# Expert blocks of a mixture-of-experts layer in pairs: first products and gelus of two blocks in one step, second products of both in the next

## The chip, the cores and the metric

The kernel runs on one core of a Trainium2 chip, as one program. The metric is the device time of one execution in microseconds (us), the median of the runs shown. Below, PE is TensorE (matrix products), DVE is VectorE, ACT is ScalarE, POOL is GpSimd and SP is SyncE, which here issues DMAs.

## The reference, cut to what matters

Two transformer layers run over x, 4 rows of 1024 tokens of width 128, in float32. The first layer (multi-query attention and a switched-head layer) is not touched by the change and fills the time up to about 2850 us. The second is:

```python
xn = _layernorm(x, axis=-1)
x = x + _L1_attn_ref(xn, ...) + _L1_ffn_ref(xn, ...)

def _favorp(data, proj, is_query):          # FAVOR attention, 16 heads, 64 features
    ...
    data_dash = jnp.einsum('bhnd,hjd->bhnj', data_normalizer * data, proj)
    diag = jnp.sum(data * data, axis=-1, keepdims=True) * (0.5 * data_normalizer * data_normalizer)
    ...                                      # stab: a maximum over the features
    return ratio * jnp.exp(data_dash - diag - stab) + EPS_FEAT

def _L1_ffn_ref(x, ...):                     # 8 experts, 2 per token, HID = 512
    logits = xf @ gate_w + gate_b
    top_w, top_i = jax.lax.top_k(logits, K)
    ...
    for e in range(E):
        h = jax.nn.gelu(xf @ w1[e] + b1[e], approximate=False)
        out = out + combine[:, e:e + 1] * (h @ w2[e] + b2[e])
    shared = jax.nn.gelu(xf @ ws1 + bs1, approximate=False) @ ws2 + bs2
    return (out + shared).reshape(orig_shape)
```

So ACT computes exps for the attention and gelus for the experts in the same stretch, and each change from one to the other needs an ACT_TABLE_LOAD.

## The kernel before, in words

**The work of the second layer.** A router has sorted the tokens by expert into blocks of 256 slots; there are 39 of them (NBLK). Of one block `j` five pieces are issued, all of them functions inside `experts()` (L1717):

- `load(j)`: SP issues the DMAs of the block's tokens xg (L1719 on) and of its expert's first weight w1. `load_second(j)`: the same of the second weight w2. All three have three buffers each.
- `turn(j)`: PE turns xg around into a PSUM tile xgT (L1739, 2 instructions), DVE copies it to SBUF (L1741), and POOL copies the columns that tell each slot's token and gate (whose, L1743; 6 buffers).
- `one(j)`: the first products pb (L1751, 8 instructions, into two PSUM tiles), and on ACT four gelus hb (L1757), two per PSUM tile. xgT and hb have two buffers each.
- `two(j)`: the second products pe (L1766, 16 instructions, one PSUM tile), two scalings yb on DVE by the gate (L1772), and two scatter-adds on POOL (L1776).

**The attention beside it.** `favor_keys(b)` (L1410) and `favor_queries(b)` (L1537) are generators, one pair per batch row. The keys: projections kp, qp (L1376), values v1p and their sum vs (L1433), diagonals dg (L1443), vsum (L1455), four groups ddk_0 to ddk_3 (L1391), the maximum over the row mxT and stab (L1481, L1488), va scaled by an exp (L1496, L1500), the products kv (L1509) and their transpose kvt (L1530). The queries: four groups ddq_0 to ddq_3, their transposes qt (L1560) with copies qfT on DVE and ACT (L1567, L1569), the outputs fo (L1578, oTf on DVE), ot (L1595), oT1p (L1614) and o1w (L1621). A group, ddq or ddk, is 16 instructions on PE into four PSUM tiles. DVE then takes four maxima of them (mq at L1545, mk at L1469) and four subtractions (qE, kE at L1401), and ACT one exp of 2048 columns (L1403).

**PSUM.** All these tiles come from one pool of eight banks of 512 columns (`small`, L76), given out in turn: a tile waits until its bank's earlier owner was read for the last time.

**The order.** In this layer PE and SP keep the order of the program (`manual_schedule`, L1214); for ACT, DVE and POOL the compiler's scheduler chooses it. The program's order is made by a loop at the end (L1818 on). It steps through the attention of row 0's keys, then row 0's queries with row 1's keys, and so on to row 3's queries, five phases in all. Each step of these generators adds a rate to `due`, and for each full 1.0 one step of a filler is issued between. The filler `fill()` (L1810) is: 13 steps of the shared expert (`shared(0, 6)`: ph with gelus, py, yT) for the first six tiles of 512 tokens, the rest of the last row of the layer before, then `experts()`, then five steps of the shared expert for the last two tiles. Behind the loop comes what is left of the filler. Last, the scatter-added sums are loaded (y) and added to x, and x is stored.

**Before the change** `experts()` has 78 steps: in iteration `j` it issues `load(j)`, `turn(j-1)`, `load_second(j-1)` and `one(j-2)` in one step, and `two(j-3)` in the next. The rates are 0.84, 0.5, 0.5, 0.5 and 1.2. With 40 attention steps in each of the three middle phases (20 of the keys and 20 of the queries), 20 filler steps, so ten blocks, go into each.

Of the kernel before, what the change touches and what calls it, by code (L numbers as in the profile page):

```python
# [58 lines left out]
NBLK = 2 * SLOTS // MB + ME - 1  # L59
# [12 lines left out]
def two_layers(ctx: ExitStack, tc: tile.TileContext, a: dict, out: bass.AP):  # L72
# [13 lines left out]
    def small(name):  # L86
        return banks.tile([P, 512], F32, tag="small", name=name)
# [262 lines left out]
    with ExitStack() as l0:  # L350
# [687 lines left out]
        def run(it):  # L1038
            for _ in it:
                pass  # L1040
# [676 lines left out]
    def experts():  # L1717
        rows_of = sorted_x.rearrange("(k q p) d -> k p q d", q=MB // P, p=P)
        loaded, seconds, turned, hidden, whose = {}, {}, {}, {}, {}  # L1719

        def load(j):
            at = nc.sync.value_load(block[0:1, 1, j : j + 1], min_val=0, max_val=ME * PER)
            xg = ff.tile([P, MB // P, ROW], F32, tag="xg", name=f"xg{j}", bufs=3)
            nc.sync.dma_start(xg, rows_of[ds(at, 1)].rearrange("o p q d -> p (o q) d"))
            e = nc.sync.value_load(block[0:1, 0, j : j + 1], min_val=0, max_val=ME - 1)
            w1 = ff.tile([P, MH], F32, tag="w1", name=f"w1_{j}", bufs=3)
            nc.sync.dma_start(w1, a["w1"][ds(e, 1)].rearrange("o d m -> d (o m)"))
            loaded[j] = xg, w1

        def load_second(j):  # L1730
            e = nc.sync.value_load(block[0:1, 0, j : j + 1], min_val=0, max_val=ME - 1)
            w2 = ff.tile([P, MHC, D], F32, tag="w2", name=f"w2_{j}", bufs=3)
            nc.sync.dma_start(w2, a["w2"][ds(e, 1)].rearrange("o (c p) d -> p (o c) d", p=P))
            seconds[j] = w2

        def turn(j):
            pt = small(f"xgT{j}")
            for q in range(MB // P):
                nc.tensor.transpose(pt[:, ts(q, P)], loaded[j][0][:, q, 0:D], ident)  # L1739
            turned[j] = ff.tile([P, MB], F32, tag="xgT", name=f"xgT{j}")  # L1740
            nc.vector.tensor_copy(turned[j], pt[:, 0:MB])  # L1741
            whose[j] = ff.tile([P, MB // P, 2], F32, tag="whose", name=f"whose{j}", bufs=6)
            nc.gpsimd.tensor_copy(whose[j], loaded[j][0][:, :, D:ROW])  # L1743

        def one(j):
            w1, xT = loaded.pop(j)[1], turned.pop(j)
            hT = hidden[j] = ff.tile([P, MHC, MB], F32, tag="hb", name=f"hb{j}")
            for c2 in range(MHC // 2):
                ph = small(f"pb{j}_{c2}")
                for k in range(2):  # L1750
                    nc.tensor.matmul(  # L1751
                        ph[:, ts(k, MB)], lhsT=w1[:, ts(2 * c2 + k, P)], rhs=xT,
                        start=True, stop=True,
                    )
                for k in range(2):
                    c = 2 * c2 + k
                    nc.scalar.activation(  # L1757
                        hT[:, c, :], ph[:, ts(k, MB)], AF.Gelu, bias=b1s[:, j, c : c + 1]
                    )

        def two(j):
            w2, hT, to = seconds.pop(j), hidden.pop(j), whose.pop(j)
            py = small(f"pe{j}")
            for q in range(MB // P):
                for c in range(MHC):
                    nc.tensor.matmul(  # L1766
                        py[:, ts(q, D)], lhsT=hT[:, c, ts(q, P)], rhs=w2[:, c, :],
                        start=(c == 0), stop=(c == MHC - 1),
                    )
            yb = ff.tile([P, MB // P, D], F32, tag="yb", name=f"yb{j}", bufs=3)  # L1770
            for q in range(MB // P):
                nc.vector.tensor_scalar(  # L1772
                    yb[:, q, :], py[:, ts(q, D)], to[:, q, 1:2], None, ALU.mult
                )

                nc.gpsimd.indirect_dma_start(  # L1776
                    out=sums[q][:, :],
                    out_offset=bass.IndirectOffsetOnAxis(
                        ap=to[:, q, 0:1].bitcast(I32), axis=0
                    ),  # L1780
                    in_=yb[:, q, :], in_offset=None, compute_op=ALU.add,
                )

        for j in range(NBLK + 3):
            if j < NBLK:
                load(j)
            if 0 <= j - 1 < NBLK:
                turn(j - 1)
            if 0 <= j - 1 < NBLK:
                load_second(j - 1)  # L1790
            if 0 <= j - 2 < NBLK:
                one(j - 2)
                yield
            if 0 <= j - 3 < NBLK:
                two(j - 3)
                yield

    def run(*its):

# [10 lines left out]
    def fill():  # L1810

        yield from shared(0, SOON)
        for _ in aside:
            pass
        yield from experts()
        yield from shared(SOON, B * T // TC)
# [1 line left out]
    filler = fill()  # L1818
    due, taken = 0.0, 0
    for k, (rows_now, rate) in enumerate((  # L1820
        ((0,), 0.84), ((0, 1), 0.5), ((1, 2), 0.5), ((2, 3), 0.5), ((3,), 1.2),
    )):
        its = [favor_queries(rows_now[0])] if k else [favor_keys(0)]
        its += [favor_keys(b) for b in rows_now[1:]]
        for _ in run(*its):
            for _ in range(3 if taken < 15 else 2):
                next(aside, None)
                taken += 1
            due += rate
            while due >= 1.0:  # L1830
                due -= 1.0
                next(filler, None)
# [78 lines left out]
```

## Time and profile before

| what | us |
|---|---|
| runs of the kernel before | 3313.93, 3315.99, 3317.91 |
| their median | 3315.99 |
| the profiled execution's own time | 3320.57 |
| its span, first to last instruction | 3318.8 |
| busy in the span: PE, DVE, ACT, POOL | 3156.9, 2413.3, 1850.8, 1899.0 |
| mean granted clock of TensorE | 0.976 |
| the stretch of the expert blocks, 2956 to 3286: length, PE busy, DVE busy, ACT busy | 330.00, 308.98, 268.09, 218.94 |
| behind it, 3286 to 3318.8: length, PE busy | 32.80, 24.65 |

How to read it: busy time is that of instructions that compute or copy; waits and DMA issues are not counted. The granted clock is the share of full speed that the throttle let TensorE have. A group of instructions is written with its line, engine, operation, and out<-in by the names in the program; behind it stand their number, busy time, mean ns of one, and the idle time of the engine just before them with what ended it. The profiled execution took 4.58 us more than the median of the runs.

### The profile page before, as it was taken

How to read it: one execution, taken by the hardware profiler on the slowest of the kernel's cores; microseconds unless marked ns; L12 is line 12 of the kernel's file. 1: busy time of each engine (PE TensorE's matmuls, PEld its weight loads, DVE VectorE, ACT ScalarE, POOL GpSimd, SP SyncE). 2: the span in 40 equal slices, each digit the busy share in tenths (PEclk: the TensorE clock that was granted, in tenths of full speed). 3: DMA queues.
4: the chain of work that ended last, by engine and by line, in shares of the span. 5: the costliest groups of instructions: out<-in, count | busy, mean ns of one | idle time of the engine just before them, and what ended most of it. 6: DMA issues, size and time to landing. Idle time of an engine off the chain costs nothing. (4 is left out here: it accounts for less than half of the span.)

```text
span 3318.8 us, 48971 instructions
## 1 busy us (share of the span) xinstructions
PE 3156.9 (95%) x15323; PEld 1714.7 (52%) x15323; DVE 2413.3 (73%) x4670; ACT 1850.8 (56%) x3273; POOL 1899.0 (57%) x2345
## 2 busy tenths in 40 slices
PE   6899999999999999999899999999999999789998
PEld 3354545555545444555454445555455554457776
DVE  7797777767777867676868776777666645658886
ACT  3345555565555555665455555656565566246675
POOL 2565555566657666666477667665767644123333
PEclk8999999999999999999999999999999999989999
DMA  5134443432323223333133232332323220024446
GB/s 152 43 97 132 132 141 98 120 108 87 94 70 99 83 79 92 95 90 90 58 95 89 84 100 83 104 87 85 93 87 93 87 76 13 12 66 89 88 88 136
DMA packets 458696, 299.77 MB, mean 90 GB/s; under 512 B 42490, under 2 KB 431108, under 8 KB 458436
## 3 DMA queue, kind: packets, MB, share of 16 engines
q1 hardware_dynamic: 412692, 225.32, 24.2%
q0 software_dynamic: 42976, 70.26, 7.7%
q8 instruction: 122, 2.00, 0.2%
q10 hardware_dynamic: 2768, 1.07, 0.1%
q14 instruction: 138, 1.13, 0.1%
HBM read 179.83 MB, written 116.26 MB: 89 GB/s over the span
## 5 line engine op out<-in xcount | busy, mean ns | idle before, releaser
L620 DVE TENSOR_REDUCE nmh<-mx 128x1 f32<-128x512 f32 x1024 | 663.8, 681 | 287.8 <-PE mx L614 286.2
L675 ACT ACTIVATE pT<-sT 128x512 f32<-128x512 f32 x1024 | 557.1, 600 | 157.6 <-PE sT L668 88.2
L874 POOL DMA_INDIRECT sorted_v<-xv,gates x464 | 469.9, 1013 | 228.0 <-DMA sorted_v<-xv,gates 129.5
L826 POOL TENSOR_TENSOR g_o<-g_o 128x256 f32<-128x256 f32 x256 | 189.4, 740 | 577.8 <-DVE g_o L825 545.6
L955 DVE TENSOR_REDUCE nms<-ps 128x1 f32<-128x1024 f32 x256 | 310.9, 1215 | 259.7 <-ACT ps L953 258.8
L950 PE MATMUL ss<-xnT,qTs 128*128 128x512 f32 x1024 | 493.2, 604 | 3.6 <-ACT qTs L820 2.0
L982 PE MATMUL cp<-pTs,vs 128*128 128x512 f32 x1024 | 460.8, 604 | 17.4 <-DVE pTs L974 11.5
L1003 PE MATMUL po<-ow,cTs 128*128 128x512 f32 x1024 | 473.1, 594 | 0.7 <-ACT cTs L987 0.7
L953 ACT COPY ps<-ss 128x512 f32<-128x512 f32 x512 | 299.3, 586 | 217.3 <-PE ss L950 213.8
L957 ACT ACTIVATE ps<-ps,nms 128x1024 f32<-128x1024 f32 x256 | 294.5, 1150 | 140.9 <-DVE nms L955 139.6
L1007 DVE TENSOR_TENSOR g_o<-po,go 128x512 f32<-128x512 f32 x512 | 333.6, 682 | 28.3 <-PE po L1003 14.1
L614 PE MATMUL mx<-ks,qs 72*128 72x512 bf16 x1024 | 312.9, 383 | 10.1 <-DVE nmh L620 4.0
L982 PEld LDWEIGHTS cp<-pTs,vs 128*128 128x128 f32 x1024 | 193.1, 194 | 243.2 <-issue 224.3
L668 PE MATMUL sT<-qs,ks 75*128 75x512 bf16 x1024 | 310.3, 383 | 7.3 <-DVE nmh L620 4.7
L950 PEld LDWEIGHTS ss<-xnT,qTs 128*128 128x128 f32 x1024 | 190.6, 192 | 182.3 <-issue 105.7
L970 PE MATMUL pTp<-ident,ps 128*128 128x128 f32 x2048 | 271.3, 275 | 13.2 <-ACT ps L957 8.8
L970 PEld LDWEIGHTS pTp<-ident,ps 128*128 128x128 f32 x2048 | 240.7, 142 | 79.6 <-issue 15.6
L926 POOL DMA_INDIRECT vs<-yv,gates x232 | 228.9, 987 | 67.4 <-issue 57.8
L926 POOL DMA_INDIRECT yg<-yv,gates x232 | 225.3, 971 | 73.4 <-issue 68.3
L987 ACT COPY cTs<-cp 128x512 f32<-128x512 f32 x64 | 37.5, 585 | 406.2 <-PE cp L982 406.2
L1003 PEld LDWEIGHTS po<-ow,cTs 128*128 128x128 f32 x1024 | 179.0, 191 | 158.3 <-issue 126.5
L658 PE MATMUL ov<-pT,va 128*32 128x512 f32 x2048 | 248.5, 603 | 0.0
(321 smaller groups left out, 4816.5 us busy)
## 6 DMA issues: line engine op xcount, KB each, us to landing
vb<-in_v_w_dram SPq DMA_DIRECT2D x667, 64.0 KB
xs<-sorted_v SPq DMA_DIRECT2D x145, 256.0 KB
yv<-xs SPq DMA_DIRECT2D x145, 256.0 KB
w<-in_w_dram SPq DMA_DIRECT2D x78, 256.0 KB
sorted_x<-nobody SPq DMA_DIRECT2D x16, 1040.0 KB
ow<-in_o_w_dram SPq DMA_DIRECT2D x32, 512.0 KB
qs<-qd SPq DMA_DIRECT2D x144, 64.0 KB
sorted_v<-xv,gates POOLq DMA_INDIRECT x464
```

The source lines that it names most:

```text
L614: nc.tensor.matmul(sc, lhsT=qs[0:NPAIR, i, ts(n, P)], rhs=ks[0:NPAIR, ts(kc, 512)], start=True, stop=True,)
L620: nc.vector.tensor_reduce(halves[:, i, n, kc : kc + 1], sc, axis=AX.X, op=ALU.max)
L668: nc.tensor.matmul(sc, lhsT=ks[:, ts(kt, P)], rhs=qs[:, i, ts(c, 512)], start=True, stop=True,)
L675: nc.scalar.activation(pT, sc, AF.Exp)
L874: nc.gpsimd.indirect_dma_start(out=sorted_v[u % 4][:, :], out_offset=bass.IndirectOffsetOnAxis(ap=column(u, k, n).bitcast(I32), axis=0), i ...
L926: nc.gpsimd.indirect_dma_start(out=to[:, n, :], out_offset=None, in_=unit[u, "y"][:, :], in_offset=bass.IndirectOffsetOnAxis(ap=column(u, ...
L950: nc.tensor.matmul(sc, lhsT=qT[:, ts(n, P)], rhs=xnT[b][:, ts(c, 512)], start=True, stop=True)
L955: nc.vector.tensor_reduce(nm, p, axis=AX.X, op=ALU.max, negate=True)
L970: nc.tensor.transpose(pt[:, ts(k, P)], p[:, ts(4 * k4 + k, P)], ident)
L982: nc.tensor.matmul(cp, lhsT=v[:, kt, :], rhs=pT[:, kt, :], start=(kt == 0), stop=(kt == NT - 1),)
L1003: nc.tensor.matmul(po, lhsT=cT[:, ts(qt, P)], rhs=unit[u, "ow"][:, ts(c, 512)], start=True, stop=True,)
L1007: nc.vector.tensor_tensor(g[:, ts(c, 4), :], po.rearrange("p (e c) -> p e c", e=4), bcast(go[:, ts(c, 4)], P), ALU.mult,)
```

## The change

The blocks are now issued in pairs. Ahead of the loop stand the loads of blocks 0 and 1, two empty steps, and a step with the turns of both. A round for blocks `j` and `j+1` has two steps. The first: `load(j+2)`, both first products with their gelus, `load(j+3)`, `load_second(j+2)`. The second: both second products, `load_second(j+3)`, and the turns of `j+2` and `j+3`. With 20 rounds (the last has one block) there are 43 steps instead of 78, and the rates of the last four phases are halved, so that ten blocks go into each middle phase as before. The buffers are as they were.

```diff
-        for j in range(NBLK + 3):
-            if j < NBLK:
-                load(j)
-            if 0 <= j - 1 < NBLK:
-                turn(j - 1)
-            if 0 <= j - 1 < NBLK:
-                load_second(j - 1)
-            if 0 <= j - 2 < NBLK:
-                one(j - 2)
-                yield
-            if 0 <= j - 3 < NBLK:
-                two(j - 3)
-                yield
+
+        def each(step, *js):
+            for j in js:
+                if 0 <= j < NBLK:
+                    step(j)
+
+        each(load, 0, 1)
+        each(load_second, 0, 1)
+        yield
+        yield
+        each(turn, 0, 1)
+        yield
+        for j in range(0, NBLK, 2):
+            each(load, j + 2)
+            each(one, j, j + 1)
+            each(load, j + 3)
+            each(load_second, j + 2)
+            yield
+            each(two, j, j + 1)
+            each(load_second, j + 3)
+            each(turn, j + 2, j + 3)
+            yield
...
-        ((0,), 0.84), ((0, 1), 0.5), ((1, 2), 0.5), ((2, 3), 0.5), ((3,), 1.2),
+        ((0,), 0.84), ((0, 1), 0.25), ((1, 2), 0.25), ((2, 3), 0.25), ((3,), 0.6),
```

## The prediction

> **What bounds the kernel now.** I read the page's first part, then the windows of the second layer, then PE's waits, its groups and the timelines. The edit touches only the stretch in which the 39 expert blocks run, 2956 to 3286 us. There PE (TensorE) is busy 308.98 of 330 us, DVE 268.09, ACT 218.94. It repeats a pattern of about 90 us, one per batch row (the third group of query products, ddq_2, starts at 2995.50, 3086.82 and 3176.56). Cut in two, two such patterns read, columns being stretch, length, busy time (instructions) of PE, PEld, DVE, ACT, POOL, granted clock, DMA:
>
> ```profile
> 2997.00:3042.00 45.00, 40.71 (x291) 30.30 (x290) 40.11 (x79) 33.98 (x40) 13.35 (x12) 0.90 0.34 72
> 3042.00:3087.00 45.00, 42.90 (x418) 37.24 (x421) 35.66 (x85) 25.84 (x39) 21.06 (x18) 1.00 0.48 105
> 3087.00:3132.00 45.00, 41.23 (x308) 30.46 (x309) 40.55 (x80) 34.23 (x40) 14.06 (x14) 0.92 0.36 73
> 3132.00:3177.00 45.00, 42.91 (x420) 37.23 (x422) 35.48 (x84) 25.84 (x39) 21.17 (x18) 1.00 0.48 105
> ```
>
> In the first half ("DVE half": ddq_2 to the last key group) PE and DVE are both nearly full, and PE runs below full clock; in the second ("PE half") PE alone is full. ACT is full in neither. Where PE stands still is in its waits (total us, times, longest):
>
> ```profile
> PE pe L1766 <- DVE xgT L1741: 6.3, 3, 2.1
> PE xgT L1739 <- ACT qfT L1569: 4.6, 3, 2.5
> PE ddk L1391 <- DVE qE L1401: 2.6, 3, 1.0
> PE pb L1751 <- DVE kE L1401: 2.4, 4, 0.7
> PE xgT L1739 <- DMA xg<-sorted_x: 1.6, 1, 1.6
> PE ot L1595 <- ACT hb L1757: 1.2, 2, 0.6
> ```
>
> Some 22 us of idle in all, half of it ended by DVE; gelus (hb) end 2.3. The groups that the edit aims at (busy, mean ns, idle before):
>
> ```profile
> L1757 ACT ACTIVATE hb<-pb,b1s 128x256 f32<-128x256 f32 x156 | 62.9, 473 | 43.3 <-PE pb L1751 42.9
> L1757 ACT ACT_TABLE_LOAD x32 | 41.1, 1283 | 22.6 <-PE pb L1751 22.4
> L1403 ACT ACT_TABLE_LOAD x28 | 35.9, 1283 | 11.7 <-issue 11.3
> ```
>
> ACT waits for PE before gelus (42.9 us), not PE for gelus.
>
> **Part 1, fewer table loads.** In the compiled order, the loads at L1403 and L1757 fall from 31 + 32 to 22 + 23 (not to 20: a pair's gelus are still split by an exp in places). 18 x 1.283 = 23.1 us of ACT leave. Of PE's idle time, ACT ends 4.6 (qfT) + 2.3 (hb) = 6.9 us. But the qfT copies are late because their exp waits for DVE ("ACT qE L1403 <- DVE qE L1401" is 26.5 us in ACT's waits), and the load in front of it is over before: at 3087.28 one starts, 4.68 of idle follow, then the exp. Bounds 0 and -6.9; I take 0.6 a pattern for three patterns, the size of one hb wait: **-1.8**.
>
> The Trainium skill, "ScalarE: Activation LUTs", "Rules for kernel authors", says to group functions by table set, as this edit does, and to budget about 2.7 us for every switch to another set; that would make 18 loads worth 48 us of ACT. In this trace an exp starts 0.02 us after its load's 1.28 us, so no more than the row is seen; by either price the time is ACT's, not PE's.
>
> **Part 2, the DVE half in the new order.** PE follows program order, so I laid after's order out with before's durations. All PSUM tiles here share 8 banks; query and key groups take 4 each and give them back only as DVE subtracts (qE, kE). Before, each of pe, xgT and pb stands between two such groups:
>
> ```profile
> 3086.82 1.15 PE L1391 MATMUL ddq<-bd,qT 32*128 32x256 f32 x16
> 3087.90 3.44 PE L1766 MATMUL pe<-w,hb 128*128 128x128 f32 x16
> 3091.26 1.48 PE L1391 MATMUL ddk<-bd,kT 32*128 32x256 f32 x16
> 3092.67 1.97 PE L1560 MATMUL qt<-ident,qE 128*128 128x128 f32 x16
> 3095.68 0.44 PE L1739 MATMUL xgT<-ident,xg 128*128 128x128 f32 x2 [1.04 <-ACT qfT L1569]
> 3096.77 1.99 PE L1751 MATMUL pb<-xgT,w 128*128 128x256 f32 x8 [0.65 <-DVE kE L1401]
> 3098.70 1.59 PE L1391 MATMUL ddq<-bd,qT 32*128 32x256 f32 x16
> ```
>
> DVE meanwhile works without a hole, four groups of 2.48 one after the other:
>
> ```profile
> 3087.99 2.48 DVE L1545 TENSOR_REDUCE mq<-ddq 128x8 f32<-128x512 f32 x4 [0.90 <-PE ddq L1391]
> 3090.73 2.48 DVE L1401 TENSOR_TENSOR qE<-ddq,mq 128x512 f32<-128x512 f32 x4
> 3093.65 2.47 DVE L1469 TENSOR_REDUCE mk<-ddk 128x8 f32<-128x512 f32 x4
> 3096.04 2.47 DVE L1401 TENSOR_TENSOR kE<-ddk,mk 128x512 f32<-128x512 f32 x4
> 3099.96 2.47 DVE L1545 TENSOR_REDUCE mq<-ddq 128x8 f32<-128x512 f32 x4
> ```
>
> After, the order is ddq_2, ddk_0, qt_1, pe, pe, xgT, xgT, ddq_3, ddk_1, fo_0, pb, pb, ... With t = 0 at ddq_2:
> - ddq_2 and ddk_0 take all 8 banks by about 3.0 (at the low clock of these rows). qt_1 needs the first bank of qE_2, which DVE frees at 1.17 + 2.48 + 0.2 + 0.6 = 4.5: PE idle 1.5.
> - qt_1 uses ddq_2's banks; the pe pair takes ddk_0's, freed from kE_0 on. DVE: qE_2 to 6.4, mk_0 to 8.9, first subtraction 9.5. qt_1 ends by about 7.1: idle 2.4.
> - pe, pe, xgT, xgT = 1.95 x 2 + 0.44 x 2 = 4.8, so ddq_3 starts at 14.3 (before: 11.88). DVE, through with kE_0, the qfT copies (1.28) and two yb pairs (1.2) by 13.2, waits about 1.9: the work that kept it full is now behind the pair.
> - fo_0 waits for ddk_1's banks and oTf (1.6, before 1.2 in two waits); ot_0 and the next pe wait for the second gelus of block 15, which ACT has placed behind an exp with its two loads (1.28 + 1.91 + 1.28): 2.5, before 0.6; qt_3 and ddk_3 come late, DVE waits 2.2.
> - DVE's chain from ddq_2 to kE_3 then takes 47.2 by this layout; in the trace it takes 45.6, 44.0 and 44.4 (mean 44.7): **+2.5** a pattern.
>
> Bounds: -1 (the 1.04 + 0.65 of idle above gone, nothing new); +5.5, if two of the gaps also cost a slow clock (pe 3.44 at 0.58, against 1.95 at full: +1.5 each). I keep 2.5, the warm layout, since this half already runs slow (0.90).
>
> On that clock: the rows show 0.60 in 3006 to 3008, after a gap of 2.45, and 0.58 in 3088 to 3090 with no gap ahead. The Trainium skill, "TensorE: Matmul & The Clock Gate", "HAM oscillation — how this bites in real kernels", asks for no PE gap over some 3.4 us; no wait here is as long, and by that rule pairing would cost no clock. The rows lower it earlier, so the upper bound stands.
>
> **Part 3, the PE half.** It gets one pb more (1.89) and one xgT less (0.44) per pattern, as 4 pe, 2 pb, 4 xgT now stand in the DVE half instead of 4, 3, 3: **+1.5**. The stall ahead of pe or dg (2.09, xgT's copy behind other DVE work) stays in another form: dg needs a bank after ddq_1 (4), pe (2), xgT (2) hold all 8: 2.7, so **+0.6**. Bounds together: 0 (the DVE half shortens by what moves out) and +2.7.
>
> Parts 2 and 3, three patterns: 3 x (2.5 + 1.5 + 0.6) = **+13.8**.
>
> **Part 4, both ends.** At the start xgT waited 1.57 for its data and pb stood before the kv products. Now the kv products come first and wait for va's multiplication (four pieces, 1.57): about 2.6, then kvt 1.2: +2.2. In the last row (queries only) pb 32 waits for xgT's copy behind mq and qE (2.0) and pe 35 for gelus behind an exp and its loads (1.7), against about 1.0 now: +2.7. At the end block 38's pe comes after fo_1, o1w_0 and ot_1 (1.92 + 1.05 + 1.04 = 4.0 later); what follows shrinks from 33.15 (3285.65 to 3318.8) to 30.7: +1.5. Sum **+6.4**; bounds 0 and +8.
>
> **DMA, SP, POOL: nothing.** The same loads are issued; xg of block j+3 waits until whose of j has been copied and both blocks' four scatters (4 x 1.57 = 6.3) stand on POOL, with some 14 us left before its turn. POOL is busy 13 to 21 of 45. If that cover went, one wait per round of a few us, three or four times a pattern, would follow.
>
> **Sum.** -1.8 + 13.8 + 6.4 = +18.4. The profiled execution took 3320.57 (span 3318.8), so it would take 3339; the median shown is 3315.99, and 3315.99 + 18.4 gives **3334**.
>
> **Rivals.**
> - *ACT was the hidden bound* (faster, chance 0.17): waits put down to DVE clear with ACT, pairs fill PE's gaps. It takes away 6.9 (ACT's idle) and 1.6 (start): -8.5, 3307. For it: gelus and exps alternate with a load each in 3098 to 3118, where ACT has almost no idle. Against: DVE's groups are back to back in the same stretch. It decides if qt_1 and the pe pair find banks at once.
> - *The pairs cost and give back the same* (within 0.2%, which is 6.6 us and about what a measurement of this kernel can tell from no change; 0.22): DVE catches up in the PE half (35.5 of 45 busy), part 2 and 3 shrink to about 1 a pattern: 3316 to 3322.
> - *Banks bound everything* (0.11): the gaps of 1.5, 2.4 and 2.5 all stay whole and two per pattern bring the low clock: 3 x (5.5 + 2.7) + 8 = +33, 3349. For it: 0.60 after a 2.45 gap.
> - *The pairing doesn't happen*: excluded for program order on PE, partial on ACT (23 loads, not 20), counted above.
>
> **Chances.** Forecast (+7 to +28) 0.50. Range: from the sum of the lower bounds (-6.9 - 3 + 0 = -9.9, 3306) to that of the upper ones (+33, 3349). Faster 0.17, same 0.22, slower 0.61.
>
> **What would show it.** Loads at L1403 + L1757 down by 18 and ACT busy down by 23; in the DVE halves PE idle ahead of qt and pe of 1.5 to 2.5, released by qE and kE; pattern length 90 to 94; kv idle at the start; last pe about 16 later. It is wrong if PE's idle in this stretch doesn't grow, or if DVE's 2.48 groups stay back to back.

## The result, and the profile after

| | us |
|---|---|
| before, median of 4 runs | 3316.95 |
| after, median of 4 runs (3356.61 to 3362.49) | 3359.51 |
| ratio after / before | 1.0121, 95% interval 1.0109 to 1.0133 |
| profiled execution after: own time, span | 3357.91, 3356.1 |
| busy in its span: PE, DVE, ACT, POOL | 3164.7, 2416.6, 1827.7, 1896.3 |

Slower, as forecast, but by 42.6 us instead of 18, and above the range. What the edit aims at came out to the digit: ACT is busy 23.1 us less (1850.8 before). Table loads of the changed kernel, from 2950 us to the end (busy, mean ns, idle before):

```profile
L1757 ACT ACT_TABLE_LOAD x23 | 29.5, 1283 | 8.6 <-PE pb L1751 8.5
L1403 ACT ACT_TABLE_LOAD x19 | 24.4, 1283 | 15.8 <-issue 15.5
```

60 loads of these two lines have become 42. Much of the loss is in PE's waits (changed kernel, 2950 us to the end; total us, times, longest):

```profile
PE dg L1443 <- DVE yb L1772: 10.7, 3, 3.7
PE ot L1595 <- ACT hb L1757: 9.3, 3, 3.1
PE qt L1560 <- DVE qE L1401: 7.9, 3, 2.7
PE fo L1578 <- DVE qE L1401: 7.7, 3, 2.6
PE pe L1766 <- issue: 5.6, 3, 2.3
PE pe L1766 <- ACT hb L1757: 3.9, 4, 1.9
PE pb L1751 <- DVE xgT L1741: 2.3, 1, 2.3
```

Of the waits shown of before only that of ot on hb is among them, grown from 1.2 to 9.3. Most come three times, once a pattern, and together they are over twice as long as the 22 us of before. I cut the two spans at the same instructions (stab of row 0, L1488, stands on PE just ahead of the expert blocks; ddq_2 is the third query group of a row, kE_3 the end of DVE's last key subtraction):

| stretch, us | before | after | change | forecast |
|---|---|---|---|---|
| start to stab of row 0 | 2955.2 | 2952.1 | -3.1 | 0 |
| stab of row 0 to the first ddq_2 | 40.3 | 41.7 | +1.4 | +2.2 |
| DVE half (ddq_2 to kE_3), three times | 45.6, 44.0, 44.5 | 47.3, 47.8, 47.5 | +8.6 | +7.5 - 1.8 |
| PE half (kE_3 to the next ddq_2), twice | 45.8, 45.8 | 53.9, 52.2 | +14.5 | +4.2 |
| third kE_3 to the last row's ddq_0 | 20.3 | 22.3 | +2.0 | +2.1 |
| last row, ddq_0 to the last pe | 44.4 | 60.6 | +16.3 | +2.7 + 4.0 |
| last pe to the end | 33.1 | 30.8 | -2.4 | -2.5 |

The sum is, but for rounding, the 37.3 us by which the spans differ. The first row is no work of the change: PE has the same instructions in both kernels up to there, and in the profiled executions of this page stab of row 0 starts anywhere from 2944.3 to 2961.5 (e17's chip apart). From stab to the end the changed kernel takes 40.4 us more (404.0 against 363.6), which is the number to set beside the 42.6 of the medians. The PE half and the last row are where the forecast is off. In the PE half, PE of the changed kernel reads:

```profile
3076.33 0.60 PE L1739 MATMUL xgT<-ident,xg 128*128 128x128 f32 x4
3080.59 2.76 PE L1443 MATMUL dg<-hsum,ksq 128*128 128x16 f32 x16 [3.66 <-DVE yb L1772]
3083.19 3.76 PE L1376 MATMUL qp<-xnT,Wq1T 128*128 128x512 f32 x4
3086.74 2.71 PE L1560 MATMUL qt<-ident,qE 128*128 128x128 f32 x16
```

and DVE in the same time:

```profile
3074.46 3.66 DVE L1433 TENSOR_REDUCE vs<-va 128x256 f32<-128x2048 f32 x1
3078.04 1.88 DVE L1545 TENSOR_REDUCE mq<-ddq 128x8 f32<-128x512 f32 x3
3079.83 0.35 DVE L1772 TENSOR_SCALAR yb<-pe,whose 128x128 f32<-128x128 f32 x1
```

PE stands still for 3.66 us, until DVE has got through vs and the maxima and reads pe's bank. Then it runs slow: dg 2.76, qp 3.76 and qt 2.71, where the kernel before shows 1.86, 1.96 and 1.91. That is 3.5 us more, nearly as much again as the gap. At the same place in the next row (gap 3.62, at 3182.27) it is 1.8 us. The granted clock (the column behind the five engines) in slices of 2 us says the same; first the changed kernel:

```profile
3080.60:3082.60 2.00, 2.00 (x14) 2.00 (x14) 2.00 (x4) 0.00 (x0) 1.70 (x2) 0.74 0.01 0
3082.60:3084.60 2.00, 2.00 (x6) 1.41 (x7) 1.71 (x6) 1.64 (x1) 1.34 (x2) 0.50 0.48 36
```

and the kernel before behind its gap of 2.09 us at the same place:

```profile
3168.50:3170.50 2.00, 1.93 (x17) 1.93 (x18) 2.00 (x6) 0.00 (x0) 0.00 (x0) 1.00 0.00 0
3170.50:3172.50 2.00, 2.00 (x21) 2.00 (x19) 2.00 (x5) 1.26 (x1) 0.00 (x0) 1.00 0.26 67
```

### The profile page after: what moved, and what is told of

It reads as the page before. It is cut to its first block, busy times and chain, and to the rows that moved or that the text cites. A ratio compares the mean times of both kernels' runs of the same rounds, so it can differ in the third digit from the quotient of the medians.

```text
span 3356.1 us, 48908 instructions
## 1 busy us (share of the span) xinstructions
PE 3164.7 (94%) x15323; PEld 1727.8 (51%) x15323; DVE 2416.6 (72%) x4670; ACT 1827.7 (54%) x3255; POOL 1896.3 (57%) x2345
## 5 line engine op out<-in xcount | busy, mean ns | idle before, releaser
L1007 DVE TENSOR_TENSOR g_o<-po,go 128x512 f32<-128x512 f32 x512 | 333.3, 681 | 28.8 <-PE po L1003 14.5
L1776 POOL DMA_INDIRECT sum<-yb,whose x78 | 122.3, 1568 | 245.5 <-DVE yb L1772 175.8
L987 ACT COPY cTs<-cp 128x512 f32<-128x512 f32 x64 | 37.5, 586 | 404.0 <-PE cp L982 404.0
```

The source lines that it names most:

```text
L1007: nc.vector.tensor_tensor(g[:, ts(c, 4), :], po.rearrange("p (e c) -> p e c", e=4), bcast(go[:, ts(c, 4)], P), ALU.mult,)
```

## The experiments

Theory A: the place of the pair's pieces on PE makes gaps, where PE meets banks that DVE still holds, and the low clock behind the gaps doubles them. Theory B: ACT, on which paired gelus make pe, ot and their followers late. Times are medians; "over before" is against the kernel before, measured beside it on the same chip. All runs but e17 lie within one level (before at 3316.5 to 3320.4); for e17, on a chip where before took 3368, the ratio is what can be compared. The half patterns are cut as above.

| run | us | over before | ratio (interval) | DVE half | PE half |
|---|---|---|---|---|---|
| before | 3316.95 | | | 44.0 to 45.6 | 45.8 |
| after | 3359.51 | +42.6 | 1.0121 (1.0109 to 1.0133) | 47.3 to 47.8 | 52.2, 53.9 |
| e1 four steps | 3341.66 | +21.2 | 1.0059 (1.0039 to 1.0080) | 43.3 to 44.0 | 51.0, 51.9 |
| e2 before, exp | 3308.86 | -11.6 | 0.9969 (0.9959 to 0.9980) | 41.6 | 45.6, 47.2 |
| e3 after, exp | 3340.38 | +19.9 | 1.0059 (1.0042 to 1.0076) | 42.0 to 44.0 | 53.6 |
| e4 shared banks | 3410.32 | +89.9 | 1.0269 (1.0252 to 1.0287) | 52.2 to 53.6 | 59.7, 62.2 |
| e5 gaps filled | 3346.65 | +30.1 | 1.0088 (1.0070 to 1.0106) | 43.6 to 46.5 | 52.0 |
| e6 shared banks, both first | 3354.83 | +38.3 | 1.0108 (1.0087 to 1.0129) | 48.5 to 49.1 | 50.2, 50.3 |
| e7 shifted | 3340.51 | +24.0 | 1.0074 (1.0052 to 1.0096) | 42.4 | 49.7, 52.8 |
| e8 one round earlier | 3355.98 | +39.5 | 1.0115 (1.0097 to 1.0133) | 47.6 to 47.8 | 53.8, 54.7 |
| e9 after without vs | 3345.14 | +24.8 | 1.0070 (1.0054 to 1.0085) | 47.8 | 47.3 |
| e10 before without vs | 3312.00 | -8.3 | 0.9970 (0.9960 to 0.9981) | 44.4 to 44.9 | 43.7 |
| e11 after, ACT in order | 3364.84 | +44.5 | 1.0134 (1.0118 to 1.0149) | 45.4 to 46.0 | 52.2 |
| e12 before, ACT in order | 3340.69 | +20.4 | 1.0062 (1.0048 to 1.0075) | 44.3 to 45.4 | 50.4 |
| e13 before, vs on POOL | 3313.28 | -7.1 | 0.9977 (0.9967 to 0.9986) | 42.4 to 44.4 | 43.9, 45.6 |
| e14 shifted, vs on POOL | 3336.32 | +15.9 | 1.0040 (1.0025 to 1.0055) | 42.8 to 44.2 | 49.2, 50.2 |
| e15 after, three causes out | 3323.20 | +2.8 | 1.0006 (0.9996 to 1.0015) | 40.9 to 44.2 | 47.7 |
| e16 before, two causes out | 3301.47 | -18.9 | 0.9938 (0.9923 to 0.9953) | 41.5 to 41.9 | 43.2 |
| e17 four causes out | 3358.06 | -10.4 | 0.9964 (0.9942 to 0.9986) | 42.5 to 44.2 | 44.3, 45.9 |

**e1: gelus paired, second products and turns apart.**

```diff
             each(one, j, j + 1)
...
             yield
-            each(two, j, j + 1)
-            each(load_second, j + 3)
+            each(two, j)
+            yield
             each(turn, j + 2, j + 3)
             yield
+            each(two, j + 1)
+            each(load_second, j + 3)
+            yield
...
-        ((0,), 0.84), ((0, 1), 0.25), ((1, 2), 0.25), ((2, 3), 0.25), ((3,), 0.6),
+        ((0,), 0.84), ((0, 1), 0.5), ((1, 2), 0.5), ((2, 3), 0.5), ((3,), 1.2),
```

> The first products and gelus of two blocks still stand in one step, as after the change, but the round has four steps at a rate of 0.5: first products of both; second products of one; turns of the next two; second products of the other. ACT keeps the paired gelus (72 table loads in the compiled program, 70 after, 88 before), while on PE each pe stands alone between two attention groups again. Theory A (the loss comes from where the pair of pe and the pair of xgT stand: PE idle ahead of qt, fo, dg and pe, with a low clock behind each gap): the time comes back to that of before, 3305 to 3325. Theory B (the paired gelus themselves are the loss, as pe and ot wait for hb): it stays at 3345 to 3360.

Between both: half of the loss goes. The DVE half is back (43.3 to 44.0), so there it is the pe pair or its place that cost; e7 tells the two apart. The PE half stays at 51 to 52: now qp waits for xgT's copy, 9.4 us in three times. Theory A holds for one half only.

**e2 and e3: no loads in the expert blocks.**

```diff
-    hT[:, c, :], ph[:, ts(k, MB)], AF.Gelu, bias=b1s[:, j, c : c + 1]
+    hT[:, c, :], ph[:, ts(k, MB)], AF.Exp, bias=b1s[:, j, c : c + 1]
```

> The kernel before with exp in place of the expert blocks' gelus, so the gelu of the routed experts is left out; every instruction stays but most table loads in this stretch go (26 in the whole program, 88 before). It measures what loads are worth at most. Theory A (ACT is off the path, only waits of PE that ACT ends can shrink, 6.9 us): 0 to -7, 3310 to 3317. Theory B (ACT bounds this stretch under cover of the other waits): -15 or more, below 3302.

> The changed kernel with exp in place of the expert blocks' gelus (the gelu of the routed experts is left out): no load stands between a pair's gelus and an exp. PE waits for hb 13.2 us in the changed kernel's trace. Theory A: at most these go, and the gaps ahead of qt, fo and dg stay (26 us): -3 to -13, 3346 to 3357. Theory B (loads and the order on ACT are the loss): back to 3330 or less.

Both gain more than theory A allowed: 11.6 before (the waits that ACT ends were 6.9), and the changed kernel's loss falls to 19.9. ACT isn't off the path, then. How a load costs PE can be read from the DVE half, first in the kernel before, then in e2 (columns as in the prediction):

```profile
3086.82:3130.79 43.97, 40.20 (x298) 29.43 (x298) 39.41 (x78) 33.22 (x40) 14.24 (x14) 0.92 0.37 75
3082.32:3123.90 41.58, 35.95 (x298) 27.10 (x298) 39.26 (x78) 19.56 (x28) 14.42 (x14) 1.00 0.40 80
```

In the three halves of e2 PE stands idle longer (16.9 us instead of 12.1), but its busy time falls from 121.9 to 107.8, at a granted clock of 1.00 instead of 0.89 to 0.92. So the gain came through rows at full clock, which no list of waits shows. Why the clock stays up without the loads is not shown.

But B doesn't hold either: with no loads in both, the changed kernel is still 31.5 us behind (19.9 + 11.6). So 11 of the 42.6 are ACT's: in e3 the waits of ot and pe on hb are gone and the DVE half (42.0 to 44.0) is as short as in the kernel before, or shorter. The PE half is untouched (53.6).

**e4 and e6: a pair in one bank.**

```diff
+        def bank(name, j):
+            if j % 2 == 0:
+                shared_bank[name] = small(f"{name}{j}")
+            return shared_bank[name][:, ts(j % 2, MB)]
...
-            pt = small(f"xgT{j}")
+            pt = bank("xgT", j)
...
-            py = small(f"pe{j}")
+            py = bank("pe", j)
```

e6 also issues both blocks' products ahead of both blocks' scalings (two_out), and both turns ahead of both copies (turn_out).

> The changed kernel with the pair's two pe in one PSUM bank and its two xgT in one (each uses 256 of 512 columns), so a round asks for 6 banks instead of 8. If the banks are what PE waits for, the waits dg <- yb (10.7 us) and pe <- issue (5.6 us) mostly go: 3340 to 3350. If the banks are only the place where PE meets DVE's backlog (maxima and vs, then subtractions), the waits move to qp or qt and the time stays within 4 us of 3359.

e4 tells nothing of the question: one tile for two blocks makes the second block's products wait until the first's were read (pe on yb 30.3 us, 11 times).

> As e4, a pair's two pe in one bank and its two xgT in one bank, but both blocks' products come before both blocks' scalings (and both turns before both copies), so that the second of a pair doesn't wait for the reading of the first, which is what made e4 slow (pe <- yb 30.3 us, xgT <- xgT 15.8). Six banks instead of eight per round. Theory banks: the wait of dg on yb (10.7 us, 3 times) goes, and with it the slow clock behind it: 3335 to 3350. Rival (PE only meets DVE's backlog there, at the next instruction): the wait moves to qp or qt, 3354 to 3364.

With that mended, dg doesn't wait any more, but qp, the group behind it, does:

```profile
PE qp L1376 <- DVE qE L1401: 5.2, 3, 1.9
```

The PE half falls by 3.6 and 1.9 us (10.7 us of waits became 5.2), the DVE half grows by 0.7 to 1.8, the time falls by 5, with intervals that overlap (1.0108 against 1.0121). Mostly the rival, then: banks are where PE meets DVE's backlog. That the backlog is the cause e9 tries.

**e5: the gaps filled with repeated work.**

```diff
+        again = name[0] == "k" and name[1:] in ("1_0", "2_0", "3_0", "1_1", "2_1", "3_1")
-        for m in range(2):
+        for m in range(2) if not again else (0, 1, 0, 1, 0, 1):
...
-            for q in range(MB // P):
+            for q in (0, 1) * (9 if j in (3, 13, 23) else 1):
                 nc.tensor.transpose(pt[:, ts(q, P)], loaded[j][0][:, q, 0:D], ident)
```

> The changed kernel with work that is repeated for nothing just ahead of three of PE's gaps in each pattern: the first and second key group (ddk_0, ddk_1, rows 1 to 3) three times instead of once (2.1 us more each, ahead of the waits of qt and fo), and the turn of blocks 3, 13 and 23 nine times (16 more transposes, 2.4 us, ahead of dg's wait). The results stay the same and nobody reads them before. Theory clock (after a gap of 2.3 us or more PE runs slow: dg 2.8 instead of 1.9, qp 3.7 instead of 2.0, pe pair 5.4 instead of 3.8): the gaps close, the rows behind them take their full-clock times, and the time falls by 8 to 20, to 3340 to 3351, though PE does some 20 us more work. Rival (DVE sets the pace there, a slow PE costs nothing): 3355 to 3364.

By the medians 12 us faster with some 16 us more work on PE (by the rows, 1.7 for each repeated key group and 1.8 for the transposes, three times): 3346.7, +30.1 instead of +42.6. The trace shows half of that in the stretch itself: from stab of row 0 to the end e5 takes 398.2 us, the changed kernel 404.0. In the DVE half of e5:

```profile
3087.22 2.77 PE L1392 MATMUL ddk<-bd,kT 32*128 32x256 f32 x48
3091.00 2.42 PE L1561 MATMUL qt<-ident,qE 128*128 128x128 f32 x16 [1.01 <-DVE qE L1402]
3095.11 3.84 PE L1767 MATMUL pe<-w,hb 128*128 128x128 f32 x32 [1.70 <-ACT qfT L1570]
3104.07 1.92 PE L1579 MATMUL fo<-qfT,kvs 128*32 128x512 f32 x16 [0.83 <-DVE qE L1402]
```

The gaps of 2.73 and 2.57 are 1.01 and 0.83, and the pe pair takes 3.84 (5.44 in the changed kernel), fo 1.92 (3.02). qt keeps its 2.42 in both, at a clock of 1.00 in this pattern: it is paced by DVE's subtractions. The half is at 43.6 in two patterns of three (46.5 in the first), with a granted clock of 1.00 there (0.89 and 0.86 in the changed kernel). In the pattern shown PE's idle time falls from 10.7 to 5.2 us, and its busy time, with the repeated work in it, rises only from 37.1 to 38.4. So the slow rows cost time, as theory clock says; but the wait of ot on hb (3.1 us) went as well, with pb earlier, so the gain isn't the clock's alone. At dg 1.95 us of gap were left, and the PE half moved little.

**e7: the same pairs at other places.**

```diff
+        if k == 1:
+            due += 0.5
```

(ahead of the steps of the second phase)

> The changed kernel with its steps issued half a step's rate earlier (due starts 0.5 higher in the second phase): the pair of pe and the pair of xgT stand between ddq_2 and ddk_0, the pair of pb behind ddq_3, as one block's pieces did before; each round stays whole. Theory A (the place between the attention groups decides, not the pairing): 3325 to 3345. Theory pairing (any whole pair costs it): 3354 or more.

In the range of theory A. The DVE half is 42.4, shorter than before the change. So a whole pair needn't cost there; the place did. What is left is in the PE half, where pb waits for dg's bank (7.1 us), and oT1p for hb (9.7 us): an exp with its two loads still parts a pair's gelus.

**e8: one round earlier.**

```diff
         each(load_second, 0, 1)
-        yield
-        yield
         each(turn, 0, 1)
```

> The changed kernel without its two empty steps at the start of the expert blocks: the same places for the same pieces, but one round (two blocks) earlier everywhere, so that no expert block is left behind the attention's last outputs. From the changed kernel's trace: the last row took 60.6 us from ddq_0 to the last pe, 44.4 before, of which some 10 are pieces of two blocks (2 pb, pe, xgT: 6.1) and attention pieces ahead of the last pe (4.0); at the start the first ddq came 7.4 earlier. If this displaced work costs time, 3347 to 3355; if it is only moved from one full stretch to another, 3356 to 3362.

The last row falls from 60.6 to 47.7 us, but from stab of row 0 to the first ddq_2 it is 6.9 longer (48.6), the tail 2.3 (33.1 again), and the two patterns are 0.3 and 2.5 longer; 3356.0 can't be told from 3359.5 by the intervals. So the 12.9 us that leave the last row come back elsewhere: they were work moved there, 9.2 of them from the start and the tail, and no loss by themselves.

**e9 and e10: without vs.**

```diff
-        nc.vector.tensor_reduce(
-            vs, va.rearrange("p n c s d -> p c s d n"), axis=AX.X, op=ALU.add
-        )
+        if b:
+            nc.vector.memset(vs, 0.0)
+        else:
+            nc.vector.tensor_reduce(
+                vs, va.rearrange("p n c s d -> p c s d n"), axis=AX.X, op=ALU.add
+            )
```

> The changed kernel without the sum of the values (vs, 3.66 us on DVE) for rows 1 to 3: vs is set to zero instead, so that this part of the computation is left out. It stands among the maxima of ddq_1 on DVE and is what dg's wait of 3.6 us ends behind. If the stretch from ddq_0 to ddq_2 is paced by DVE's work and PE pays for the gap a second time in slow rows behind it (dg, qp, qt: 3.5 us), the time falls by 3 x (3.6 + 2 to 3.5) = 17 to 21, to 3338 to 3343. If the gap costs only itself: 3347 to 3349. If other work is late there anyway: 3355 or more.

> The same edit (vs of rows 1 to 3 set to zero, its sum left out) in the kernel before, where pe waits at this place for xgT's copy (6.3 us in three times) and the rows behind run at full clock. Expected from the waits: -5 to -7, 3310 to 3312, a third of what the changed kernel gains. If DVE's work as such were the pace of the stretch, it would gain as much as the changed kernel, 3 x 3.66 = 11 or more: 3306 or less.

The loss falls by 17.8 (42.6 to 24.8) for three reductions of 3.66 us, in the range for a gap paid twice; 3345.1 itself lies between the ranges, as the kernel before was 3.4 us slower beside it. The kernel before gains 8.3, more than its waits and half as much, not a third. The traces part the two more clearly. The PE half gives back 5.7 in the mean (53.0 to 47.3) against 2.0 before, which is just the wait there (2.1); the first of the three reductions, between stab of row 0 and the first ddq_2, gives back 5.0 (41.7 to 36.7) against 2.0. PE in e9 at the place:

```profile
3076.83 1.93 PE L1446 MATMUL dg<-hsum,ksq 128*128 128x16 f32 x16 [0.46 <-DVE qE L1401]
3078.61 1.96 PE L1376 MATMUL qp<-xnT,Wq1T 128*128 128x512 f32 x4
3080.41 1.91 PE L1563 MATMUL qt<-ident,qE 128*128 128x128 f32 x16
```

The gap is 0.46 and the three rows behind it are back at full speed.

**e11 and e12: ACT in program order.**

```diff
-        tc.manual_schedule(engines={mybir.EngineType.PE, mybir.EngineType.SP})
+        tc.manual_schedule(
+            engines={mybir.EngineType.PE, mybir.EngineType.SP, mybir.EngineType.Activation}
+        )
```

> The changed kernel with ACT in the program's order too, instead of the scheduler's: a pair's eight gelus stay together (62 table loads in the compiled program, 70 after). The wait of ot on hb (9.3 us in three times), which comes from an exp with its two loads inside a pair's gelus, should go; pe may wait for gelus behind kE_1's exp in its place. Theory A: -3 to -12, 3347 to 3357. If the order on ACT were most of the loss: below 3335. If head-of-line waiting on ACT costs more than it gives: above 3362.

> The kernel before with ACT in the program's order: a block's four gelus stay together, and of neighbouring exps (qE, kE) one follows the other without a load between (78 table loads in the compiled program, 88 before, 70 after), with PE's order untouched. e2 took 11.6 us off by dropping nearly all loads of this stretch, 62 of them; ten fewer are worth a sixth of it, 2, and the unsplit gelus up to 2.3 more (PE's waits for hb): 3312 to 3317. If ACT's waiting in order costs more: 3320 or above.

Two misses. In e11 ot's wait is gone, but pe waits 8.6 us for hb, o1w 3.5 for oT, and the last row takes 67.9. In e12, with fewer loads and PE's order as before, xgT waits 6.8 us (no releaser shown; in this order the qfT copies on ACT, which free banks, stand behind the exp of kE) and qp 7.7. What fewer loads are worth by themselves can't be seen here, as ACT's other work was held back for them; that it is the copies which hold PE is read from the order, not tried.

**e13 and e14: vs on POOL, an exact version.**

```diff
+            nc.gpsimd.tensor_tensor(vs, va[:, 0], va[:, 1], ALU.add)
+            for n in range(2, NT):
+                nc.gpsimd.tensor_tensor(vs, vs, va[:, n], ALU.add)
```

(for rows 1 to 3, in place of the reduction on DVE)

> The kernel before with the sum of the values (vs) of rows 1 to 3 on POOL, as seven additions of 256 columns, in place of one reduction of 3.66 us on DVE; the result is the same. Leaving vs out took the kernel before from 3320.3 to 3312.0. If POOL (13 to 21 of 45 us busy here) has it done before vsum asks for it: 3310 to 3316. If POOL's queue (scatter-adds, whose) makes it or the scatters late: 3320 or above.

0.9977 (0.9967 to 0.9986): faster than both kernels. From the first ddq_2 to the end its trace is 5.2 us shorter than that of before; ahead of it, from stab of row 0 on, it is 4.2 longer, as xgT waits 5.4 us for its data there. POOL in e13:

```profile
3070.65 1.31 POOL L1434 TENSOR_TENSOR vs<-va 128x256 f32<-128x256 f32 x1
3072.03 4.77 POOL L1436 TENSOR_TENSOR vs<-vs,va 128x256 f32<-128x256 f32 x6
```

It is done at 3076.8; vsum asks for it at 3081.73.

> The pairs at the places of e7, with vs of rows 1 to 3 on POOL as in e13. In e7 the DVE half took 42.4 us a pattern (44.0 before, 47.8 after the change), the PE half 50 to 53 (45.8 before), with pb waiting 2.7 us for dg behind DVE's vs. If that wait and the slow rows behind it go with vs: the PE half falls to 45 to 47, and the time from 3340 by 10 to 16, to 3324 to 3331. If the gelus split by an exp (3.2 us, oT1p <- hb) hold it: above 3335.

pb no longer waits for dg, but 3336.3 is at the other expectation: the split gelus (oT1p <- hb, 9.7 us, as in e7) hold the PE half at 49 to 50. Here vsum also waits for the sum on POOL, 2.9 us in two times.

**e15 to e17: do the causes add up?** e15 is the changed kernel with e3's, e9's and e8's edits, e16 the kernel before with e2's and e10's, e17 is e15 with e7's.

> Closure: the changed kernel with exp for the experts' gelus (no loads between), without vs in rows 1 to 3, and without the two empty steps at the start. It leaves out the gelu of the routed experts and this sum. If the loss of 42 us is a gelu pair that an exp splits, DVE's backlog at dg, and work displaced to the end, this comes near e16, the kernel before with the same parts left out: within 12 us. If the pairing costs by itself: 25 or more above e16. From e3 (DVE half 42.0, -19) and e9 (PE half 47.3, -17) and e8 (-3): 3318 to 3325.

> The kernel before with exp for the experts' gelus and without vs in rows 1 to 3, to be set beside e15. From e2 (-11.6) and e10 (-8.3), if they add: 3299 to 3303. If both free the same wait: 3306 to 3309.

> e15 with the steps shifted as in e7, so that the pairs of pe and xgT stand between ddq_2 and ddk_0 instead of behind both (gelu of the routed experts and the sum vs of rows 1 to 3 are left out, no empty steps at the start). In e15 the waits of qt and fo on qE (2.7 and 2.6 us a pattern, with slow rows behind: pe 5.9 instead of 3.8, fo 3.5 instead of 1.9) and of pe are what is left, 7 us a pattern over e16. If this place is the fourth and last cause: 3301 to 3311, within 10 us of e16. If a pair costs in any place: 3315 or more.

e16 is where two gains that add should be. e15, though in its range, stands 21.7 us above e16: between the two expectations, so something was left. e15's waits name it:

```profile
PE qt L1563 <- DVE qE L1401: 8.2, 3, 2.7
PE fo L1581 <- DVE qE L1401: 7.7, 3, 2.6
```

e17, where the pairs stand between the groups, doesn't have these waits, and is 8.5 us above e16 (-10.4 against -18.9); the intervals of the two ratios just overlap. The traces agree: on e17's chip stab of row 0 starts some 50 us later (3002.9), but from there to the end e17 takes 357.1 us, 8.2 more than e16 (348.9). Whether a pair costs these last us in any place stays open.

## Why the prediction was wrong

The direction and most mechanisms were right, two terms were far too small: part 3 and part 4. From stab of row 0 on, the spans differ by 40.4 us where the sum has 18.4. Of the 22 us between them 10.2 lie in the rows that part 3 forecast, 8.9 in part 4's and 2.9 in those of parts 1 and 2. By its own steps:

- *Part 1, loads (-1.8).* The count (18) and ACT's busy time (-23.1) are exact. The worth of a load was bounded too tightly by the waits that ACT ends (6.9): e2 gains 11.6 in the kernel before, through faster rows and not through waits. But the change made a wait of its own there, as an exp still parts one pair's gelus in each pattern (ot <- hb 9.3 us). Of the 42.6 us, 11 go when the loads go in both kernels (31.5 is left).
- *Part 2, the DVE half (+2.5 a pattern).* Right: +2.9 (8.6 by three, with part 1's term in it), and the waits came where the layout put them, at their longest qt 2.7 (forecast 1.5), pe 2.3 (2.4), fo 2.6 (1.6), ot 3.1 (2.5). That the sum came out is partly luck: the two groups ahead of qt took 2.0 us, not 3.0, and the pe pair 5.3 to 5.4, not 3.9. The slow clock, which stood in the text only as an upper bound, is a good part of the cost: in e5 and e7 the granted clock of this half is 0.96 to 1.00 (0.86 to 0.89 after the change), and the half is down to 42.4 to 43.6 in all but e5's first pattern.
- *Part 3, the PE half (+1.5 + 0.6, bounds 0 to +2.7).* This is the step that failed. Measured is +8.1 and +6.4. The text put dg's stall at 2.7 us against 2.1; it is 3.66 and 3.62, and behind it dg, qp and qt lose 3.5 us to the clock in the first of the two halves and 1.8 in the second, which the text didn't count in this half at all. The 2.09 us of before, at the same place, were followed by none. With the pieces moved in (1.5, as forecast), the longer gap (1.6) and waits of pe on hb and of stab that the text didn't have (1.1), the rows explain 7.7 and 5.9; the two halves differ by just what their slow rows do. e9 and e10 show it: the same 3.66 us of DVE work are worth 5.7 us a PE half after the change and 2.0 before. The cause named, eight banks held, was only half right: with banks to spare (e6) PE stops at qp for the same backlog.
- *Part 4, both ends (+6.4).* This failed too. Measured +15.3 (+1.4 + 16.3 - 2.4). The two empty steps at the start move a round of blocks from the start to the last row. The text priced the waits at the start but didn't credit the work that leaves it, nor charge it to the last row; nor did it count dg's stall there, which the start has as well (3.44 us, with slow rows). In e8, where the round is moved back, both ends cost 8.3 + 3.3 us over before; 5.0 of that is the longer gap and the slow rows at dg, part 3's term, and the other 6.6 are close to the forecast's sum. The time falls by no more than the runs can tell.
- *DMA, SP, POOL: nothing.* Right: no such wait is among PE's.
- *The rivals.* "Banks bound everything", at +33 and 0.11, came nearest, since it alone charged the low clock behind its gaps; but it did so only in the DVE half, and what PE waited for was DVE's work, not the number of banks. "ACT was the hidden bound" is wrong for this change, but e2 shows that the kernel before had some of it, through the clock.

In pairs of kernels with the same parts left out, the loss goes from 42.6 to 31.5 without loads (e3, e2), to 33.1 without vs (e9, e10), to 21.7 without both and with the round moved back (e15, e16), to 8.5 with another place for the pairs (e17, e16). The last rests on two chips. From stab of row 0 on, the traces give 40.4, 32.1, 29.7, 18.7 and 8.2.

## What to carry to other kernels

Price a wait on a full TensorE by what follows it, not by its length alone: look in the profile at how long a gap at that place was before, and whether the rows behind it were slow, and count both. When pieces that were spread out are joined, first lay out the one engine that frees their buffers: in the half that the forecast had most wrong it wasn't the count of banks, nor the number of table loads, but one reduction of 3.66 us on DVE. Moving that to an engine with room (e13) took 7.1 us off the kernel before, more than 18 of the 62 loads that e2 drops would be worth if each were worth the same (11.6 x 18 / 62 = 3.4, an estimate). And before two traces are compared from their start, look whether they agree up to where the change begins.

## What the runs showed of the hardware

- No length of a single gap tells in these traces whether the granted clock falls. It stayed at 1.00 behind gaps of 2.09 us (before, 3168.57) and 2.30 (after, 3277.65). It fell to 0.50 behind gaps of 2.57 (fo), 3.09 (ot) and 3.66 us (dg), from 0.4 us ahead of the next row's start to 1.7 us behind it, and was back at 1.00 some 3 to 7 us later. Behind one gap of 2.73 (3099.71) it was still 1.00 for the next 2 us, and fell when a second gap of 2.32 followed 2.4 us of work later; behind an equal one (3199.73) it fell within 1.3 us. It also fell behind a gap of 1.86 (after, 3302.11), and in the kernel before with none in the 8 us ahead (0.50 in 3089 to 3091); the same rows stand ahead of that place in e2, where it stays at 1.00. What decides it stays open. The Trainium skill, "TensorE: Matmul & The Clock Gate", "HAM oscillation — how this bites in real kernels", names gaps of more than some 3.4 us. Here shorter ones did it too, so the rows decide.
- On PE, repeated work for nothing in gaps made the kernel 12 us faster by the medians (e5), 5.8 by the traces from stab of row 0 on.
- Two blocks in one PSUM bank as one tile make each other wait in this program, unless all writes come before all reads: 51 us more in e4 than in the changed kernel, 5 less in e6 (not clear of noise).
- Seven additions on POOL took 6.1 us for what one DVE reduction does in 3.66. In e13 nothing on PE waited for them, in e14 vsum did.
